# A transformer block with conditioning on one core: another order and other products in its front

## The chip, the cores and the metric

The kernel runs on one core of a Trainium2 chip. The metric is the time of one execution on the device in microseconds. The engines are named as the profile names them: PE (TensorE; PEld are its weight loads), DVE (VectorE), ACT (ScalarE), POOL (GpSimd) and SP (SyncE, which here only issues DMAs). A product in float32 on PE appears in the trace as two records.

## The reference

Two batches of 2048 tokens with 576 channels go through one block with 16 heads of 36 channels. A conditioning vector per batch gives six vectors (shift, scale and gate for the attention, shift, scale and gate for the MLP).

```python
ada = jax.nn.silu(c) @ W_ada + b_ada
shift_msa, scale_msa, gate_msa, shift_mlp, scale_mlp, gate_mlp = jnp.split(ada, 6, axis=-1)
h = _modulate(_layernorm(x), shift_msa, scale_msa)
x = x + gate_msa * _attention(h, W_qkv, b_qkv, W_proj, b_proj)
h = _modulate(_layernorm(x), shift_mlp, scale_mlp)
mlp = jax.nn.gelu(h @ W_fc1 + b_fc1, approximate=True) @ W_fc2 + b_fc2
x = x + gate_mlp * mlp
```

`_modulate(x, shift, scale)` is `x * (1 + scale) + shift`. Everything is float32.

## The kernel before

The kernel has a front and a main part. Each engine runs its instructions in the order in which the program gives them.

**The front** (lines 141 to 427) makes queries, keys and values of batch 0 and everything that comes from the conditioning. Channels are cut in five pieces of 128 (`kc`, the last with 64 channels and a row for the bias), tokens in four stages of 512 (`tb`). A stage is the generator `queries_keys_values` (L175): it loads four tiles of x (L180), takes mean and variance and normalizes them on DVE (L102 to L127, L190), turns them on PE so that channels lie on partitions (`pt`, L201), applies scale and shift while leaving PSUM (L136 on ACT, L138 on DVE) into `hT`, multiplies 9 tiles of queries and keys (`pq`, L208, 128 x 512, five products each) and four tiles of values (`pv`, L231), and stores them to `qk_d` and `v_d` in DRAM through SP's queue (L223, L248).

The conditioning comes from `c_in` (Silu, L265), turned into `cT` (five pieces with two columns, one per batch), and from W_ada, of which a sixth of 576 columns is one `wa` (`load_ada`, 1.33 MB, two buffers). `modulation(part)` (L282) makes scale or shift with the channels on partitions: for each of five output pieces and five `kc` one product with 128 x 128 weights of `wa` and the two columns of `cT` moving (`pa`, L288). `gates(part)` (L309) makes a gate with the same row on all partitions: weights `c_bc`, which is `cT` of one batch spread over 128 columns, and 288 columns of `wa` moving (`pg`, L318), ten products per batch. Parts 0 and 1 (shift and scale of the attention) are needed before the first `hT`; 2 and 5 are gates; 3 and 4 belong to the MLP. The gates then multiply W_proj and W_fc2, which go back to DRAM (`gated`, L335).

The order is written by hand: `next(stages[n])` advances a stage by one step, and the generator `later` (L363) is advanced once per tile of `pq` or `pv`, so that its work lies between them (L406 to L425). x is loaded through ACT's queue, W_ada through SP's, the first third of W_qkv (`w_in`) through POOL's and the others through SP's.

**The main part** (from L432) runs 128 units (one head of one block of 512 queries), each in four groups `G` of 256 + 256 keys: scores `s` (L496), copies to `e` (ACT, L509), maxima (DVE, L514), subtraction (L551), Exp (L555) and the product with the values `av` (L567). Scores run eight groups ahead of `av`. Beside this attention lies filling work, in steps of about 4 to 6 us of PE: `tokens` and `projections` for batch 1 (four times 512 tokens, `pq_q` L770, `pv_q` L732, their loads on POOL's queue), then for each finished block of queries its projection (`po` L887) and the MLP (`pf` L956 and L970, `py` L1020). `fill` takes steps from the list `work`. It is forced in every group before the first `av`, afterwards in every even group, and in an odd one if a credit allows it: the credit gains 2.55 in each group, loses the cost of each step, and starts at -10. Turns of tokens are `lights`: small steps, two of which may go into a group without a fill. At the start of the main part the first 512 tokens of batch 1 are normalized at once (L1075, with loads L636 and the norm L656 on ACT); their turns (`pt_q`, L677) are the first fills.

Of the kernel before, what the change touches and what calls it, by code (L numbers as in the profile page):

```python
# [10 lines left out]
F32 = mybir.dt.float32  # L11
# [11 lines left out]
def dit_block_kernel(  # L23
# [35 lines left out]
    def seq(ins):  # L59

        return tc.keep_in_program_order(ins)

    def rows(kc):
        return P if kc < KC - 1 else KL + 1
# [68 lines left out]
    def modulated(dst, pt, norm, kc, b, on_act):  # L133
# [3 lines left out]
        else:  # L137
            seq(nc.vector.tensor_scalar(dst, pt, sc, sh, op0=ALU.mult, op1=ALU.add))  # L138


    with ExitStack() as front:
        enter = front.enter_context
# [8 lines left out]

        evp = enter(tc.tile_pool(name="ev", bufs=4))
        wq_p = enter(tc.tile_pool(name="wqkv", bufs=1))
        hp = enter(tc.tile_pool(name="h", bufs=2))
        lnp = enter(tc.tile_pool(name="ln", bufs=4))
        ap = enter(tc.tile_pool(name="ada", bufs=1))
        awp = enter(tc.tile_pool(name="ada_w", bufs=2))
# [17 lines left out]
        def queries_keys_values(b, tb):  # L175
            mvs = lnp.tile([P, TB, nc.vector.BN_AGGR_DIM], F32, tag="mv", name=f"mv_{b}_{tb}", bufs=2)
            xts, xns = [], []
            for i in range(TB):
                xt = lnp.tile([P, C], F32, tag="xt", name=f"xt_{b}_{tb}_{i}", bufs=8)
                seq(nc.scalar.dma_start(out=xt, in_=x[b, ts(tb * TB + i, P), :]))  # L180
                xts.append(xt)
            yield
            for i in range(TB):
# [10 lines left out]
                )  # L194
                xns.append(xn)
            yield
            hT = hp.tile([P, KC, QB], F32, tag="hT", name=f"hT_{b}_{tb}")
            for kc in range(KC):
                pt = bank(f"pt_{b}_{tb}_{kc}")
                for i in range(TB):  # L200
                    seq(nc.tensor.transpose(pt[:, ts(i, P)], xns[i][:, ts(kc, P)], ident))  # L201
                modulated(hT[:, kc, :], pt, 0, kc, b, kc % 2 == 1)
            yield
            for m in range(2 * C // P):
                pq = bank(f"pq_{b}_{tb}_{m}")
                for kc in range(KC):
                    seq(
                        nc.tensor.matmul(  # L208
                            pq,
                            lhsT=w_in[: rows(kc), kc, ts(m, P)],  # L210
                            rhs=hT[: rows(kc), kc, :],
                            start=(kc == 0),
                            stop=(kc == KC - 1),
                        )
                    )
                ev = evp.tile([P, QB], F32, tag="ev", name=f"ev_{b}_{tb}_{m}")
                if m < C // P:
                    seq(nc.scalar.mul(ev, pq, SCALE))
                elif m == C // P:
                    seq(nc.vector.tensor_scalar_mul(ev, pq, qscale))  # L220
                else:
                    seq(nc.vector.tensor_copy(ev, pq))
                seq(nc.sync.dma_start(out=qk_d[b][ts(m, P), ts(tb, QB)], in_=ev))  # L223
                yield
            for i in range(TB):
                t = tb * TB + i
# [21 lines left out]
                seq(nc.sync.dma_start(out=v_d[b][ts(t, P), :], in_=vt.rearrange("p h e -> p (h e)")))  # L248
                yield

        stages = [queries_keys_values(0, tb) for tb in range(NQB)]
        next(stages[0])
        was = {0: load_ada(0), 1: load_ada(1)}
        w_in = wq_p.tile([P, KC, 3 * C], F32, name="w_in")
        main, last = pieces(w_qkv)
        for n in range(3):
            cols = ts(n, C)
            to = w_in[:, :, cols]
            by = nc.sync if n else nc.gpsimd
            seq(by.dma_start(out=to[:, 0 : KC - 1, :], in_=main[:, :, cols]))  # L260
            seq(by.dma_start(out=to[0:KL, KC - 1, :], in_=last[:, cols]))
            seq(by.dma_start(out=to[KL : KL + 1, KC - 1, :], in_=b_qkv[cols].unsqueeze(0)))
        next(stages[1])

        seq(nc.scalar.activation(c_in[:, 0:C], c_raw, AF.Silu))  # L265
        pt = bank("pt_c")
        for kc in range(KC):
            seq(nc.tensor.transpose(pt[:, ts(kc, B)], c_in[:, ts(kc, P)], ident[:B, :B]))
        cT = ap.tile([P, KC, B], F32, name="cT")
        seq(nc.vector.tensor_copy(cT.rearrange("p k b -> p (k b)"), pt[:, 0 : KC * B]))  # L270
        c_bc = ap.tile([P, B, KC, P], F32, name="c_bc")
        for b in range(B):
            for kc in range(KC):
                seq(
                    nc.vector.tensor_copy(
                        c_bc[:, b, kc, :], cT[:, kc, b : b + 1].to_broadcast([P, P])
                    )
                )

        def modulation(part):  # L280

            wa = was.pop(part)  # L282
            pa = bank(f"pa_{part}")
            for fc in range(KC):
                m = P if fc < KC - 1 else KL
                for kc in range(KC):
                    seq(
                        nc.tensor.matmul(  # L288
                            pa[:m, ts(fc, B)],
                            lhsT=wa[: rows(kc), kc, ds(fc * P, m)],  # L290
                            rhs=cT[: rows(kc), kc, :],
                            start=(kc == 0),
                            stop=(kc == KC - 1),
                        )
                    )
            to = 2 * (part // 3) + (1 - part % 3)
            add = 1.0 if part % 3 == 1 else 0.0
            spans = [(0, P, 0, KC - 1), (0, KL, KC - 1, KC)]
            if part // 3:
                spans.append((64, KL, KC - 1, KC))  # L300
            for at, m, lo, hi in spans:
                seq(
                    nc.vector.tensor_scalar_add(
                        mod[at : at + m, to, lo:hi, :].rearrange("p k b -> p (k b)"),
                        pa[:m, lo * B : hi * B],
                        add,
                    )
                )

        def gates(part, made):  # L310

            wa = was.pop(part)
            for b in range(B):
                pg = wide(f"pg_{part}_{b}")
                for n in range(2):
                    for kc in range(KC):
                        seq(
                            nc.tensor.matmul(  # L318
                                pg[:, n, :C2],
                                lhsT=c_bc[: rows(kc), b, kc, :],  # L320
                                rhs=wa[: rows(kc), kc, ts(n, C2)],
                                start=(kc == 0),
                                stop=(kc == KC - 1),
                            )
                        )
                g = ap.tile([P, C], F32, name=f"gate_{part}_{b}")
                seq(
                    nc.vector.tensor_copy(
# [1 line left out]
                    )  # L330
                )
                made.append(g)
                yield

        def gated(jobs):  # L335

# [27 lines left out]
        def later():  # L364
# [38 lines left out]
                at = slice(f, f + 3)  # L403
                jobs.append((src[:, at, :], P, 3, half, [d[:, at, :] for d in dsts]))
            yield from gated(jobs)
            modulation(3)  # L406
            yield
            modulation(4)

        next(stages[0])  # L410
        modulation(0)
        modulation(1)
        rest = later()
        next(rest)
        next(stages[0])
        for n, stage in enumerate(stages):
            if n + 2 < NQB:
                next(stages[n + 2])
            if n + 1 < NQB:
                next(stages[n + 1])  # L420
            for i, _ in enumerate(stage):
                next(rest, None)
                if i == 6 and n + 1 < NQB:
                    next(stages[n + 1])
        for _ in rest:  # L425
            pass
# [5 lines left out]
    with ExitStack() as main_part:  # L432
# [4 lines left out]
        ps_f = pool("ps_f", 2, space=PSUM)  # L437
        ps_v = pool("ps_v", 1, space=PSUM)
        ep = pool("e", 9)
        kp = pool("k", 2)  # L440
        np_ = pool("n", 2)
        bp = pool("blk", 2)
        mp = pool("mlp", 2)
# [2 lines left out]
        class Unit:  # L446
# [6 lines left out]
                self.es = {}  # L453

            def load_keys(self):
                u, b, h = self.u, self.b, self.h
                self.kT = kp.tile([P, HALF], F32, tag="kT", name=f"kT_{u}")
                self.qT = kp.tile([P, QB], F32, tag="qT", name=f"qT_{u}")
                for i in range(2):
                    at = ds(64 * i, D)  # L460
                    seq(
                        nc.sync.dma_start(
                            out=self.kT[at, :], in_=qk_d[b][ds(C + h * D, D), ts(i, HALF)]
                        )
                    )
                    seq(
                        nc.sync.dma_start(
                            out=self.qT[at, :], in_=qk_d[b][ds(h * D, D), ts(self.qb, QB)]
                        )
                    )  # L470

            def load_values(self):
                self.v = kp.tile([P, L // P * HA + 64 - HA], F32, tag="v", name=f"v_{self.u}")
                nt = L // P * HA
                seq(nc.vector.memset(self.v[:, nt:], 0.0))
                seq(
# [192 lines left out]

        def turned(key, xns, norm, b):  # L670

            h2 = bp.tile([P, KC, QB], F32, tag="big", name=f"h_{key}")

            def piece(kc):
                pt = room(f"pt_{key}_{kc}", 1)[0]
# [5 lines left out]


        lights = []
        ready = {}

        def lit():

# [134 lines left out]
        def gather(k):  # L822

            sums = bp.tile([P, H * QB // P], F32, tag="sums", name=f"sums_{k}")
            seq(nc.gpsimd.dma_start(out=sums, in_=flat_rows(sum_d[k])))
            oT = bp.tile([P, KC, QB], F32, tag="big", name=f"oT_{k}")
            outs[k] = oT
            seq(
                nc.gpsimd.dma_start(
# [239 lines left out]
        AHEAD = 2 * NG  # L1069
        RATE = 2.55  # L1070
        lasts = []
        work = [[tokens(1, tb), projections(1, tb), None] for tb in range(NQB)]
        credit = -10.0
        state["busy"] = True
        units[0].load_keys()  # L1075
        while work[0][0] is not None:
            if next(work[0][0], 0) == 0:
                work[0][0] = None

        def advance():  # L1080

# [149 lines left out]
```

## Time and profile before

| | us |
|---|---|
| median of 3 runs | 3847.03 (3845.86 to 3847.26) |
| the profiled execution: its time | 3850.33 |
| its span, on which the views below stand | 3848.6 |
| mean granted clock of PE | 0.991 |

"Span" is the time from the first to the last instruction in the trace. A busy time is the sum over the instructions of an engine. The chain is followed back from the last instruction: at each step to what released it. "Issue" in it is time in which the engine waited for nothing that the profile shows. The granted clock says which share of its full speed PE had.

### The profile page before, as it was taken

Reading aid. Unit: us, or ns where it says so; the run is one execution under the profiler, and the core shown is the slowest. Engines: PE = TensorE matmul, PEld = TensorE weight load, DVE = VectorE, ACT = ScalarE, POOL = GpSimd, SP = SyncE. Lnnn points to the kernel's source line nnn. Section 1 sums busy time; section 2 is a strip of 40 time slices with the busy share of each in tenths; the row PEclk is TensorE's granted clock in tenths of the full one; section 3 lists DMA queues with packets and bytes.
Section 4 is the critical chain, followed back from the end, with each engine's and each line's share of the span. In section 5 each row is a group of like instructions: output and inputs, shape, how many; then the busy total and the mean of one; then the engine's idle time right before and its main releaser. Section 6 shows DMA issues by size and latency. Waiting matters only on the chain.

```text
span 3848.6 us, 58305 instructions
## 1 busy us (share of the span) xinstructions
PE 3791.6 (99%) x23533; PEld 1806.7 (47%) x23533; DVE 2936.6 (76%) x2983; ACT 2340.9 (61%) x2203; POOL 568.5 (15%) x821
## 2 busy tenths in 40 slices
PE   8999999999999999999999999999999999999998
PEld 5554434444344444444444534454444444444555
DVE  2514787878888988898888898888888888888421
ACT  0003776766766776676776676667666767677321
POOL 0210111111111011111111021112110111011211
PEclk9998999999999999999999999999999999999999
DMA  5732443344444343343343343434342434243321
GB/s 167 255 136 69 87 99 94 87 116 88 104 86 93 69 95 85 85 88 88 69 102 90 70 112 69 99 71 105 74 102 63 105 80 93 68 102 63 104 82 57
DMA packets 415473, 362.60 MB, mean 94 GB/s; under 512 B 312762, under 2 KB 312762, under 8 KB 415204
## 3 DMA queue, kind: packets, MB, share of 16 engines
q1 hardware_dynamic: 350900, 173.37, 22.8%
q0 software_dynamic: 62000, 180.78, 15.6%
q10 hardware_dynamic: 2304, 4.72, 0.4%
q8 instruction: 186, 3.05, 0.4%
q14 instruction: 83, 0.68, 0.1%
HBM read 287.52 MB, written 71.21 MB: 93 GB/s over the span
## 4 chain that ended last, share of the span: by engine, by line
PE 93%; issue 4%; DMA 1%; DVE 1%; POOL 1%; ACT 0%; SPq 0%; POOLq 0%; ACTq 0%
PE av L567 23%; PE s L496 23%; PE py L1020 13%; PE pf L970 12%; PE pq_q L770 4%; PE pq L208 4%; PE po L887 4%; PE pv_q L732 2%; PE pv L231 2%; PE pf L956 2%; PE mt L532 2%; PE pa L288 1%; PE pg L318 1%; PE pt_b L677 0%; PE pt_q L677 0%
## 5 line engine op out<-in xcount | busy, mean ns | idle before, releaser
L509 ACT COPY e<-s 128x1024 f32<-128x1024 f32 x1024 | 989.7, 1024 | 690.4 <-PE s L496 688.7
L551 DVE TENSOR_TENSOR e<-e,m 128x2048 f32<-128x2048 f32 x512 | 1162.2, 2274 | 7.4 <-DMA m<-m_d 7.4
L514 DVE TENSOR_TENSOR acc<-acc,e 128x1024 f32<-128x1024 f32 x768 | 939.0, 1223 | 213.1 <-ACT e L509 169.0
L555 ACT ACTIVATE e<-e 128x2048 f32<-128x2048 f32 x512 | 992.0, 1938 | 9.4 <-DVE e L551 9.4
L567 PE MATMUL av<-e,v 64*64 64x512 f32 x8192 | 981.8, 594 | 0.6 <-DVE up L580 0.6
L496 PE MATMUL s<-qT,kT 36*64 36x512 f32 x8192 | 979.0, 592 | 0.8 <-ACT vt L245 0.8
L1020 PE MATMUL py<-w,gT 128*128 128x288 f32 x2304 | 585.1, 412 | 6.7 <-DVE gT L1000 3.5
L496 PEld LDWEIGHTS s<-qT,kT 36*64 36x64 f32 x8192 | 311.0, 133 | 561.7 <-issue 519.8
L567 PEld LDWEIGHTS av<-e,v 64*64 64x64 f32 x8192 | 291.5, 132 | 525.5 <-issue 475.5
L970 PE MATMUL pf<-h_b,w_b 128*128 128x512 f32 x1152 | 532.1, 606 | 4.4 <-DMA w_b<-in_L_cond_W_fc_dram 4.4
L1020 PEld LDWEIGHTS py<-w,gT 128*128 128x128 f32 x2304 | 434.4, 191 | 184.9 <-issue 36.8
L588 POOL DMA_DIRECT2D o_d<-up x128 | 110.0, 859 | 2239.2 <-DMA o_d<-up 1286.1
L970 PEld LDWEIGHTS pf<-h_b,w_b 128*128 128x128 f32 x1152 | 208.5, 190 | 323.6 <-issue 308.1
L542 DVE TENSOR_REDUCE mx<-mt 128x4 f32<-128x512 f32 x128 | 88.2, 689 | 200.5 <-PE mt L532 199.8
L981 ACT ACTIVATE gT<-pf,b 128x512 f32<-128x512 f32 x144 | 99.0, 687 | 189.7 <-PE pf L956 131.5
L887 PE MATMUL po<-wpr_p,oT 128*128 128x288 f32 (+1 forms) x640 | 167.9, 419 | 6.3 <-DVE x_b L899 6.3
L770 PE MATMUL pq_q<-h_q,w_q 128*128 128x512 f32 (+1 forms) x360 | 167.0, 611 | 6.5 <-DMA w_q<-in_L_cond_W_qkv_dram 6.5
L208 PE MATMUL pq<-hT,w_in 128*128 128x512 f32 (+1 forms) x360 | 161.8, 607 | 0.3 <-ACT hT L136 0.2
L514 DVE TENSOR_TENSOR acc<-e 128x1024 f32<-128x1024 f32 x128 | 155.4, 1214 | 4.7 <-ACT e L509 4.7
L992 DVE SCALAR_TENSOR_TENSOR th<-th,gT 128x1024 f32<-128x1024 f32 x72 | 88.1, 1223 | 90.9 <-ACT th L990 90.7
L887 PEld LDWEIGHTS po<-wpr_p,oT 128*128 128x128 f32 (+1 forms) x640 | 122.3, 195 | 62.4 <-issue 11.0
L1032 DVE TENSOR_TENSOR x_b<-py,x_b 128x288 f32<-128x288 f32 x192 | 81.5, 451 | 85.9 <-PE py L1020 85.8
(136 smaller groups left out, 2336.0 us busy)
## 6 DMA issues: line engine op xcount, KB each, us to landing
w<-w_d POOLq DMA_DIRECT2D x72, 576.0 KB, 6.2
v<-v_d SPq DMA_DIRECT2D x128, 296.0 KB
kT<-qk_d SPq DMA_DIRECT2D x256, 144.0 KB
w_b<-in_L_cond_W_fc_dram POOLq DMA_DIRECT2D x72, 512.0 KB, 4.5
m<-m_d SPq DMA_DIRECT2D x128, 256.0 KB
qT<-qk_d SPq DMA_DIRECT2D x256, 72.0 KB
w_d<-wg POOLq DMA_DIRECT2D x12, 864.0 KB, 6.3
qk_d<-ev SPq DMA_DIRECT2D x36, 256.0 KB
```

The costliest lines, as they stand in the source:

```text
L208: nc.tensor.matmul(pq, lhsT=w_in[: rows(kc), kc, ts(m, P)], rhs=hT[: rows(kc), kc, :], start=(kc == 0), stop=(kc == KC - 1),)
L496: nc.tensor.matmul(s[ts(c, 64), i, :], lhsT=self.kT[at, ds((2 * g + j) * P + 64 * c, 64)], rhs=self.qT[at, :], start=True, stop=True,)
L509: seq(nc.scalar.copy(self.es[g][:, j], s))
L514: top = lambda out, x, y: seq(nc.vector.tensor_max(out, x, y))
L551: seq(nc.vector.tensor_sub(e, e, m))
L555: seq(nc.scalar.activation(e, e, AF.Exp))
L567: nc.tensor.matmul(self.av[ts(i, 64), r, :], lhsT=self.v[ts(r, 64), ds((c + i * (HALF // P)) * HA, 64)], rhs=e[ts(r, 64), j, i, :], start= ...
L588: seq(nc.gpsimd.dma_start(out=o, in_=hi[1:HA, :], accum_op=ALU.add))
L770: nc.tensor.matmul(pq, lhsT=w[: rows(kc), kc, ts(j, P)], rhs=hT[: rows(kc), kc, :], start=(kc == 0), stop=(kc == KC - 1),)
L887: nc.tensor.matmul(po[n][:, :C2], lhsT=oT[: rows(kc), kc, ts(i, P)], rhs=wpr[: rows(kc), kc, ts(n, C2)], start=(kc == 0), stop=(kc == KC - 1),
L970: nc.tensor.matmul(pfs[j], lhsT=w1[:, kc, ts(j, P)], rhs=h2[:, kc, :], start=(kc == 0 and j == 0), stop=(kc == KC - 2 and j == 1),)
L1020: nc.tensor.matmul(py[n][:, :C2], lhsT=gTs[f - f % 2][:, f % 2, ts(i, P)], rhs=w2s[f - f % 2][:, f % 2, ts(n, C2)], start=(j == 0), stop=( ...
```

## The change

**The first loads.** x of the first two stages goes through SP's queue instead of ACT's, and so does the first third of `w_in` instead of POOL's. SP's order is then: the conditioning vector, x of stage 0, W_ada 0 and 1, `w_in` 0 and 1, x of stage 1, `w_in` 2, W_ada 2 and 5.

**The products of the conditioning.** `rows_of(part)` takes the two columns of `cT` as weights and 288 columns of `wa` as the moving side; the result is two rows (one per batch). The pieces `kc` 0 to 3 go to partitions 0, 32, 64 and 96 of the PSUM tile, so to four strips of 32 columns of PE; `kc` 4 is added to the first. The tile is cleared on DVE first, and copied to SBUF afterwards (`rows`). `modulation` then adds the strips up and turns the rows by five products with `rows` as weights and the two columns of `of_b` moving (`pm`). `gates` spreads them over all partitions by one product per half and batch with the weights `spread[b]`. `c_bc` goes.

**The order.** Between the rows of parts 0 and 1 and their `pm` the first two turns of stage 0 are issued. A gate takes the same number of steps of `later` as before (rows, then both batches); parts 3 and 4 take four steps instead of two. A fifth stage, `queries_keys_values(1, 0)`, is advanced up to its `hT`: the first 512 tokens of batch 1 are loaded (ACT's queue), normalized (DVE) and turned within the stages of the front, and the main part begins with `projections(1, 0)` without turns. The keys and queries of unit 0 are loaded after the last tile of `pq`. The buffers of `hT` and of the later `h` and `oT` are now one pool, as are the keys of the front and of the main part.

The diff, cut:

```diff
+    kp = ctx.enter_context(tc.tile_pool(name="k", bufs=2))
+    hp = ctx.enter_context(tc.tile_pool(name="h", bufs=2))
+    def load_keys(u):
...
-                seq(nc.scalar.dma_start(out=xt, in_=x[b, ts(tb * TB + i, P), :]))
+                by = nc.sync if (b, tb) in ((0, 0), (0, 1)) else nc.scalar
+                seq(by.dma_start(out=xt, in_=x[b, ts(tb * TB + i, P), :]))
...
+            pts = []
+            if (b, tb) == (0, 0):
+                pts = [turn(kc) for kc in range(2)]
+                yield
+            for kc in range(KC):
+                pt = pts[kc] if kc < len(pts) else turn(kc)
                 modulated(hT[:, kc, :], pt, 0, kc, b, kc % 2 == 1)
...
+                if m == 2 * C // P - 1 and tb == NQB - 1:
+                    first_keys.extend(load_keys(0))
...
-        stages = [queries_keys_values(0, tb) for tb in range(NQB)]
+        stages = [queries_keys_values(0, tb) for tb in range(NQB)] + [queries_keys_values(1, 0)]
         next(stages[0])
         was = {0: load_ada(0), 1: load_ada(1)}
...
+        load_in(0)
+        load_in(1)
         next(stages[1])
+        load_in(2)
+        NC = P // 32
+        of_b = ap.tile([P, B], F32, name="of_b")
+        nc.vector.tensor_reduce(
+            out=of_b,
+            in_=ident.rearrange("p (k q) -> p q k", k=NC)[:, 0:B, :],
+            op=ALU.add,
+            axis=AX.X,
+        )
+        def cleared(part):
+            pa = wide(f"pa_{part}")
+            seq(nc.vector.memset(pa[:, :, :C2], 0.0))
+            return pa
+        pas = {part: cleared(part) for part in range(2)}
...
+        def rows_of(part):
+            wa = was.pop(part)
+            pa = pas.pop(part) if part in pas else cleared(part)
+            for n in range(2):
+                for kc in range(KC):
+                    at = 32 * (kc % NC)
+                    seq(
+                        nc.tensor.matmul(
+                            pa[at : at + B, n, :C2],
+                            lhsT=cT[: rows(kc), kc, :],
+                            rhs=wa[: rows(kc), kc, ts(n, C2)],
+                            start=(kc < NC),
+                            stop=(kc == KC - 1 or 0 < kc < NC),
+                        )
+                    )
+            t = ap.tile([P, C], F32, tag="rows", name=f"rows_{part}", bufs=2)
+            seq(nc.vector.tensor_copy(t.rearrange("p (n c) -> p n c", n=2), pa[:, :, :C2]))
+            return t
+        def modulation(part, t):
+            pm = wide(f"pm_{part}")[:, 0, :]
             for fc in range(KC):
                 m = P if fc < KC - 1 else KL
-                for kc in range(KC):
-                    seq(
-                        nc.tensor.matmul(
-                            pa[:m, ts(fc, B)],
-                            lhsT=wa[: rows(kc), kc, ds(fc * P, m)],
-                            rhs=cT[: rows(kc), kc, :],
+                seq(
+                    nc.tensor.matmul(
+                        pm[:m, ts(fc, B)], lhsT=t[:, ds(fc * P, m)], rhs=of_b, start=True, stop=True
...
         def gates(part, made):
-            wa = was.pop(part)
+            t = rows_of(part)
+            yield
             for b in range(B):
                 pg = wide(f"pg_{part}_{b}")
                 for n in range(2):
-                    for kc in range(KC):
-                                lhsT=c_bc[: rows(kc), b, kc, :],
-                                rhs=wa[: rows(kc), kc, ts(n, C2)],
+                            pg[:, n, :C2], lhsT=spread[b], rhs=t[:, ts(n, C2)], start=True, stop=True
...
-            modulation(3)
-            yield
-            modulation(4)
+            for part in (3, 4):
+                t = rows_of(part)
+                yield
+                modulation(part, t)
         next(stages[0])
-        modulation(0)
-        modulation(1)
+        ts_ = [rows_of(part) for part in range(2)]
+        next(stages[0])
+        for part in range(2):
+            modulation(part, ts_[part])
+        for b in range(B):
+            seq(nc.vector.tensor_copy(spread[b], of_b[:, b : b + 1].to_broadcast([P, P])))
...
-        for n, stage in enumerate(stages):
-            if n + 2 < NQB:
+        for n in range(NQB):
+            if n + 2 <= NQB:
                 next(stages[n + 2])
-            if n + 1 < NQB:
-                next(stages[n + 1])
-            for i, _ in enumerate(stage):
+            next(stages[n + 1])
+            for i, _ in enumerate(stages[n]):
                 next(rest, None)
-                if i == 6 and n + 1 < NQB:
+                if i == 6:
                     next(stages[n + 1])
...
-        ready = {}
+        ready = {"q1_0": (hTs[1, 0], [])}
...
-        work = [[tokens(1, tb), projections(1, tb), None] for tb in range(NQB)]
+        work = [[tokens(1, tb) if tb else None, projections(1, tb), None] for tb in range(NQB)]
         credit = -10.0
         state["busy"] = True
-        units[0].load_keys()
-        while work[0][0] is not None:
-            if next(work[0][0], 0) == 0:
-                work[0][0] = None
+        units[0].kT, units[0].qT = first_keys
```

## The prediction

> **What bounds the kernel now.** First the page: its busy times, its clock row and the shares of the chain. TensorE is busy for all but 57 us.
>
> ```profile
> PE 3791.6 (99%) x23533; PEld 1806.7 (47%) x23533; DVE 2936.6 (76%) x2983; ACT 2340.9 (61%) x2203; POOL 568.5 (15%) x821
> ...
> PEclk9998999999999999999999999999999999999999
> ...
> PE 93%; issue 4%; DMA 1%; DVE 1%; POOL 1%; ACT 0%; SPq 0%; POOLq 0%; ACTq 0%
> ```
>
> So time is won only by giving PE less to do, by letting it start sooner, or by a higher clock. The change touches the front (to 323 us) and the first steps of the attention, so second I read the chain there, in order of time (start, length, what).
>
> ```profile
> 1.16 10.58 DMA wa<-in_L_cond_W_ada_dram
> 12.13 1.28 ACT L265
> ...
> 15.17 19.64 PE pa L288 x100
> ...
> 39.74 17.30 PE pq L208 x40
> 57.04 4.86 PE pg L318 x20
> ...
> 205.95 5.57 PE pa L288 x50
> 211.52 7.20 PE pq L208 x10
> 218.72 7.88 PE pa L288 x50
> 227.04 6.15 issue
> ...
> 327.26 1.62 ACT xn_q L656 x2
> ...
> 344.06 5.79 PE pq_q L770 x10
> 349.86 1.88 PE s L496 x16
> ```
>
> To see: the first useful product, pq, starts at 39.7 us; 100 narrow records of pa stand before it; pa for the MLP's parts takes 13.5 us around 206; the first pq_q of batch 1 starts 21 us after the front's end (the last pv ends at 323.4). Third, the windows of those stretches (width, PE busy and records, the other engines, granted clock, DMA share, GB/s).
>
> ```profile
> 206.00:207.00 1.00, 1.00 (x11) 1.00 (x10) 0.75 (x1) 0.00 (x0) 0.00 (x0) 1.00 1.06 389
> ...
> 212.00:213.00 1.00, 1.00 (x2) 0.33 (x1) 0.00 (x0) 0.00 (x0) 0.00 (x0) 0.50 0.00 0
> ```
>
> ```profile
> 335.00:340.00 5.00, 5.00 (x23) 1.85 (x22) 2.41 (x2) 3.06 (x4) 0.00 (x0) 0.50 0.00 0
> ```
>
> To see: pa runs 11 records in 1 us at clock 1.00; after 4.5 us of it the clock is 0.50, and the pq behind it takes 7.2 us instead of 4.29. The clock is 0.50 again from 326 to 346 us, as attention starts. In the windows from 16 to 24 us pa makes only 11 records in 2 us: half rate too, although no throttle is recorded yet.
>
> **Part A, the start: 10.9 us.** Today pa waits for the Silu, which stands on ScalarE behind the eight xt issues until 12.1 us. Those move to SP's queue. There the order is now c_raw, four xt (1.18 MB), wa 0, wa 1, w_in 0 (1.33 MB each), so each queue entry counts. The windows give 0.59 MB in the first 4 us and then 349 GB/s on average to 32 us (324 with SP's queue alone, 28 to 32 us, so one queue suffices): wa 0 has landed at 9.5 us, wa 1 at 13.3, w_in 0 at 17.1. VectorE clears two banks, copies cT at about 6 us and needs 8.5 us for the norm (today 16.5 to 25.0): 14.6 us. The new rows product of a part has 10 matmuls of 288 columns, 20 records; pg shows 0.243 us each (4.86/20). The four kc groups lie in four column strips. If strips overlap as the 64x64 tiles do (16 records of 512 in 1.72 us, 0.43 each in pq: fourfold), the longest strip holds 8 records, 1.94 us, and at half clock 3.9. I take half clock: rows end at 13.4 and 17.3 us. Then two turns (1.05), 20 narrow pm records at 0.182 (3.6) and the additions (0.4): 22.4; three turns and their modulations remain of today's 4.8 us, about 3.9: pq at 26.3, 13.4 us earlier. From that I take 2.5 us, because today's pq starts at full clock and here it follows narrow records (the 7.20 above is 2.9 too long). The copies of rows (0.76 like gate) lie beside turns. Bounds: serial strips at half clock, 9.7 us per part, put pq at 37.9, and with that slow pq the part loses 0.7; full clock throughout leaves wa 1 as the bound, pq at 22.8 us and 16.9 gained. I take 10.9, since av shows that strips with different moving data overlap.
>
> **Part B, the gates: 10.9 us.** Today 4 x 4.86 = 19.4 us of pg. After: two rows products, 2 x 1.94, four spreads of 4 records, 4 x 0.97: 7.8. [...] Six parts switch, two of them here: 0.7. [...] If strips are serial it is 5.1. Clears and copies are on VectorE (0.76 each for the copies; it is busy for 10 of the 50 us from 50 on), and each pg waits until after the next pq, 4.3 us, which covers the copy; without the cover 0.8 us each.
>
> **Part C, parts 3 and 4: 11.6 us.** From 205.95 to the next turn at 232.94 lie 27.0 us. After: two pq, 8.6; two rows, 3.9; 20 pm records at 0.11, 2.2; switches 0.7: 15.4. This rests on the clock staying up. [...] Here PE is not idle at all and is still throttled, after 4.5 us of two-column products. [...] Serial strips give 5.8, with the drops staying 3.
>
> **Part D, the first tokens of batch 1: 9.7 us.** Today from 323.36 to 349.79 us PE does four groups of s, 20 transposes and one pq_q: 26.4 us, waiting for the norm on VectorE and ScalarE (to 328.9 us) and at half clock. After: 0.83 us of wait for the last vt copy as today, 4 x 1.88, 4.29, and the transposes now in the front at the 4.05 us that the stage at 232.94 needs: 16.7. The norm, 8.5 us on VectorE, moves beside pv and pq of the third stage (VectorE has 4 of 50 us there; uncovered it would cost 8.5). Its four loads go from POOL's to ScalarE's queue; behind them wait evictions of pq, as behind the xt loads of every stage today. POOL is rid of those and of w_in 0; wpr and w_q follow earlier, hidden. On SP, kT and qT of unit 0 now wait for the last qk_d store ahead of the v_d stores, some 2 us (v_d lands in 2.11); v is read over 20 us later, so nothing waits. The first e copy waits for the last v_d store today too. If the clock drops anyway, D is 5.
>
> **The rest.** Three fill slots (five lights) leave the loop. Set side by side, the two instruction orders show fills 3 to 6 steps early at first; the credit takes this back, and from the second third of block 0 on the lead is 0 to 2, the last av beside the same piece of block 6. I set the rest at nothing, with 6 us either way: the 6.5 us wait of pq_q for w_q between the first two token blocks should go, since its POOL neighbours change, and an equal one come between the second and third.
>
> Sum 10.9 + 10.9 + 11.6 + 9.7 = 43.1. The profiled execution took 3850.3 us with 1.7 outside the span of 3848.6; it would become 3807.2. It is 3.3 above the median of 3847.0, so 3804 for the median.
>
> **Rivals.** Serial strips (20%): 128-row strips might share one stream, as every row feeds four. For it, no row shows this shape; against it, av. Then -0.7 + 5.1 + 5.8 + 9.7 = 19.9: 3827. Throttle stays (15%): products with two weight columns might count as idle whatever they stream; for it the half rate from 16 us on, against it that pa streamed only two columns. A 7, B 9, C 4, D 8: 28, so 3819. Slower (6%): the moved phase of fills against units lets each of the 128 unit ends wait for an eviction, as it now does now and then (av for up 0.6, pt_q for vt_q 0.6 us). At 0.6 each that is 77 us: 3881; it decides from 0.34 us per unit end (43.1/128). Against it: the credit restores the phase. The gains eaten by several small waits: 4%, 3845.
>
> **How the numbers follow.** My case has 55%, 3804, and its own bounds 3795 to 3815. The range takes in both middle rivals: 3792 to 3828. Measurement tells 0.2% (7.7 us). Faster 0.90 (55 + 20 + 15), same 0.04, slower 0.06.
>
> **What would show it.** A: first pq near 26 us, and rows records overlapping (20 in about 2 to 4 us). B: pg groups of 1 us. C: clock 1.00 around the two pm groups and no stretch of pq above 4.5 us. D: first pq_q within 4 us of the last pv, clock 1.00. I am wrong if rows takes 4.86 us or more, if the clock rows still show 0.50 in the front, or if PE's idle time after 350 us grows.

## The result, and the profile after

The changed kernel takes 3804.28 us (median of 4 runs, 3802.73 to 3805.81), the kernel before, on the same chip, 3847.15 (4 runs, 3845.86 to 3850.51): ratio 0.9885, 95% interval 0.9869 to 0.9901. A second comparison on another chip gave 0.9880 (0.9863 to 0.9896). The forecast was 3804. The profiled span fell from 3848.6 to 3802.8 us, by 45.8; the profiled execution of the kernel before was 3.2 us slower than the median of its kernel, that of the changed kernel 0.3.

The page after, the lines that answer to those shown of before (busy times, clock row, shares of the chain):

```profile
PE 3748.3 (99%) x23429; PEld 1762.1 (46%) x23429; DVE 2946.1 (77%) x2995; ACT 2335.5 (61%) x2196; POOL 564.7 (15%) x814
...
PEclk9999999999999999999999999999999999999999
...
PE 93%; issue 4%; DVE 1%; ACT 1%; DMA 1%; POOL 0%; POOLq 0%; SPq 0%; ACTq 0%; DVEq 0%
```

To see: TensorE's busy time fell by 43.3 us, the rest of the span by 2.5 (57.0 to 54.5). The change gives TensorE less to do and a faster clock (mean granted 0.995, before 0.991); TensorE still bounds the kernel (93% of the chain).

The chain of the changed kernel in order of time (start, length, what):

```profile
11.36 6.30 PE pa L331 x40
17.66 1.02 PE pt L218 x8
18.68 2.20 PE pm L349 x20
...
24.63 17.89 PE pq L233 x40
42.52 2.04 PE pa L331 x20
...
49.05 1.94 PE pg L375 x8
...
55.30 1.53 issue
56.83 2.10 PE pa L331 x20
...
181.97 1.59 issue
183.57 2.11 PE pa L331 x20
185.67 4.49 PE pq L233 x10
190.16 1.01 PE pm L349 x10
191.17 1.17 issue
192.34 3.28 PE pa L331 x20
195.62 4.96 PE pq L233 x10
...
298.44 4.49 PE pq_q L812 x10
```

To see: the first pq starts at 24.6 us and not at 39.7. A rows group of 20 records takes 2.04 to 2.11 us. The first pq_q of batch 1 starts 2.9 us after the front's end (295.56; s waits 0.83 us from there). And three pieces called issue, 1.53, 1.59 and 1.17 us, stand ahead of rows groups: no step of the prediction has them. The last rows group (3.28) and the pq behind it (4.96) are slow. A window there shows why, clock 0.56 (width, PE busy and records, the other engines, granted clock, DMA share, GB/s):

```profile
193.00:194.00 1.00, 1.00 (x12) 0.23 (x3) 0.00 (x0) 0.00 (x0) 0.00 (x0) 0.56 0.00 0
```

The parts of the forecast against the two profiled executions, in us gained:

| part | forecast | profile | how the profile's number is made |
|---|---|---|---|
| A, the start | 10.9 | 14.5 | pq from 39.74 to 24.63, less 0.6 for its first 40 records (17.30 to 17.89) |
| B, the gates | 10.9 | 9.5 | 57.04 to 89.37 is 32.3; 42.52 to 65.38 is 22.9 |
| C, parts 3 and 4 | 11.6 | 7.4 | 205.95 to 232.94 is 27.0; 181.97 to 201.58 is 19.6 |
| D, first tokens of batch 1 | 9.7 | 9.6 | 26.4 against 12.9 for the same work after the front and 3.9 for the turns in it |
| the rest | 0 (6 either way) | 4.8 | 45.8 less the four |

The total is within 3 us of the difference of the spans, but through terms that were off by up to 4.8 us in both directions. The experiments ask about each.

### The profile page after: what moved, and what is told of

It reads as the page before. It is cut to its first block, busy times and chain, and to the rows that moved or that the text cites. A ratio compares the mean times of both kernels' runs of the same rounds, so it can differ in the third digit from the quotient of the medians.

```text
span 3802.8 us, 58130 instructions
## 1 busy us (share of the span) xinstructions
PE 3748.3 (99%) x23429; PEld 1762.1 (46%) x23429; DVE 2946.1 (77%) x2995; ACT 2335.5 (61%) x2196; POOL 564.7 (15%) x814
## 3 DMA queue, kind: packets, MB, share of 16 engines
q0 software_dynamic: 61328, 178.27, 15.4%
## 4 chain that ended last, share of the span: by engine, by line
PE 93%; issue 4%; DVE 1%; ACT 1%; DMA 1%; POOL 0%; POOLq 0%; SPq 0%; ACTq 0%; DVEq 0%
PE av L609 23%; PE s L538 23%; PE py L1062 13%; PE pf L1012 13%; PE pq_q L812 4%; PE pq L233 4%; PE po L929 4%; PE pv_q L774 2%; PE pf L998 2%; PE pv L258 2%; PE mt L574 2%; PE pa L331 0%; PE pt_b L719 0%; ACT e L551 0%; DMA o_d<-up 0%
## 5 line engine op out<-in xcount | busy, mean ns | idle before, releaser
L631 POOL DMA_DIRECT2D sum_d<-up x128 | 143.6, 1122 | 0.0
```

What stands on the lines that cost most here:

```text
L631: seq(nc.gpsimd.dma_start(out=sums, in_=hi[0:1, :], accum_op=ALU.add))
```

## The experiments

Each kernel is the changed one with one edit, unless it says otherwise. A ratio to the kernel before has an interval of about 0.0015 either way, some 6 us; smaller differences are read from the traces. Most runs were on other chips than the first comparison, so the ratios are what compares; "above the changed kernel" means above 3804.28.

**Do the strips stream beside each other?** In rows_of all five kc groups go to one strip:

```diff
-                    at = 32 * (kc % NC)
+                    at = 0
...
-                            start=(kc < NC),
-                            stop=(kc == KC - 1 or 0 < kc < NC),
+                            start=(kc == 0),
+                            stop=(kc == KC - 1),
```

> The changed kernel, with all five kc groups of a rows product in one column strip, one after the other (the other three strips hold the zeros of the clear, so the sum is the same). My theory: a rows group of 20 records takes 2.1 us after the change because the four strips stream beside each other; on one strip each record takes the 0.243 us of pg, a group 4.86 us: 2.8 us more for each of parts 2, 5, 3 and 4 (11 us), and 8 to 13 us more at the start, where part 0 runs at half clock: 19 to 24 us above the changed kernel, 3824 to 3828. The rival, that the records are short because their weights have only two columns: a group stays at 2.1 us and the time at 3804.

Measured: 3821.82 us, ratio 0.9931 (0.9914 to 0.9947), 17.5 above the changed kernel. From its chain:

```profile
48.40 4.95 PE pa L331 x20
...
65.62 6.70 PE pa L331 x20
```

To see: the same 20 records take 4.95 us, 0.248 each like pg's, and 6.70 where the clock falls inside them (0.66, 0.50, 0.50 and 0.63 in the four windows from 66 to 70 us). Parts 3 and 4 take 5.01 and 6.70. The weights are as narrow as before, so the short group comes of the four strips side by side; the rival falls. The start loses 5.5 us (first pq at 30.13) and the four later groups 2.9, 4.6, 2.9 and 3.4: 19.3, and the first s of attention stands at 315.64, 19.25 later. The whole span differs by 17.3.

**The three waits named issue.** The timeline of the changed kernel at the second of them (start, length, engine, line, what, and in brackets the idle time before it):

```profile
182.06 0.75 DVE L245 TENSOR_SCALAR ev<-pq,qscale 128x512 f32<-128x512 f32 x1 [5.21 <-PE pq L233]
...
182.93 0.54 DVE L313 MEMSET pa<- 128x576 f32 x1
...
183.57 2.11 PE L331 MATMUL pa<-wa,cT 128*2 128x288 f32 x20 [1.61 <-issue]
```

To see: VectorE had waited 5.21 us for the pq tile, evicts it, and only then clears the bank, because `cleared(part)` stands behind that eviction in its queue; TensorE waits for both. The edit clears one step earlier, ahead of the eviction:

```diff
@@ gates(part, made, clear=None); part 2 is called with clear=5
+            if clear is not None:
+                pas[clear] = cleared(clear)
             yield
@@ later()
-            yield from gated(jobs)
+            steps = 2 + B * len(jobs)
+            for i, _ in enumerate(gated(jobs)):
+                if i == steps - 1:
+                    pas[3] = cleared(3)
+                yield
             for part in (3, 4):
                 t = rows_of(part)
+                if part == 3:
+                    pas[4] = cleared(4)
                 yield
```

> The changed kernel, with the clears of the PSUM tiles of parts 5, 3 and 4 one step earlier on VectorE's queue: ahead of the eviction of the pq tile that TensorE is still computing, not behind it. My theory: TensorE's waits of 1.53, 1.59 and 1.17 us before the rows of these parts are the 0.69 to 0.75 us eviction, the 0.54 us memset and their semaphores; all three go, 4.3 us; and if the clock drop from 192 to 198 us came of 1.0 us of pm, the 1.2 us wait and 2.1 us of rows in a row, it goes too, 1.6 us more: 3798 to 3800. Rival: TensorE waits there for something else (the bank, or the weights of the part from memory): no gain, 3804. The clock drop may stay, since pm and rows still follow each other: then 3800.

Measured: 3796.72 us, ratio 0.9864 (0.9849 to 0.9878). From its chain, parts 3 and 4:

```profile
182.85 4.49 PE pq L233 x10
187.34 0.99 PE pm L349 x10
188.33 2.04 PE pa L331 x20
190.37 4.49 PE pq L233 x10
```

To see: no issue piece stands between pm and rows, none is left ahead of the other two groups either (51.45 pq for 4.29 us, 55.74 rows), and rows and pq of part 4 are back at 2.04 and 4.49. Parts 3 and 4 now take 15.0 us (180.81 to 195.85), where the forecast had 15.4. So C's missing 4.2 us were these waits and the clock drop behind them. That the drop needs the wait is shown by more than one pair: in all five traced executions that have the wait ahead of part 4's rows (the changed kernel twice, serial strips, D taken out, old loads) the clock falls to 0.50 as it ends or within 1.3 us of that, in none of the four with early clears and single pm products. The first s of attention starts at 290.67 and not 296.39, although the first pq of this run was 0.44 later: 6.2 us from the clears.

**Part D taken out**: the first tokens of batch 1 are again normed and turned at the start of attention.

```diff
-        stages = [queries_keys_values(0, tb) for tb in range(NQB)] + [queries_keys_values(1, 0)]
+        stages = [queries_keys_values(0, tb) for tb in range(NQB)]
...
-        ready = {"q1_0": (hTs[1, 0], [])}
+        ready = {}
...
+        while work[0][0] is not None:
+            if next(work[0][0], 0) == 0:
+                work[0][0] = None
```

> The changed kernel without the first tokens of batch 1 in the front: they are normed and turned at the start of attention, as before the change; unit 0's keys are still loaded early. My theory: the front ends 3.9 us earlier and from its end to the end of the first pq_q group it takes about 26 us again, not 17, with clock 0.50: 9 to 13 us above the changed kernel, 3813 to 3817. The wait of pq_q for w_q falls between the first and the second token block again, about as long as now. A rival for the 4 to 5 us that were gained after the first blocks and that no part of my sum named: if they come of the phase that part D changed, they go too: 3818 to 3822, and the four waits of po for x_b (6.3 us) are back.

Measured: 3819.34 us, ratio 0.9923 (0.9908 to 0.9937), 15 above the changed kernel: the rival's number. From its table of waits (engine, line, for what: us in total, times, longest):

```profile
PE po L930 <- DVE x_b L942: 6.3, 4, 1.6
...
PE py L1063 <- DVE x_b L1075: 3.1, 2, 1.6
```

The po line of the pages of the kernel before and of the changed one (busy, mean ns, idle before it and what ended that):

```profile
L887 PE MATMUL po<-wpr_p,oT 128*128 128x288 f32 (+1 forms) x640 | 167.9, 419 | 6.3 <-DVE x_b L899 6.3
...
L929 PE MATMUL po<-wpr_p,oT 128*128 128x288 f32 (+1 forms) x640 | 163.0, 410 | 0.1
```

To see: the four waits of po and the two of py are back exactly as in the kernel before (6.3 and 3.1); in the changed kernel po does not wait for x_b at all, and py 1.6 us once. The clock is at half again as attention starts (10.0 us lost from 296 to 318 us), and the wait for w_q, 7.0 us, stands ahead of the third token block, not the second as I had written. So these waits come and go with D: with it, the fill steps meet the attention units at another phase, and the first steps of po no longer wait for VectorE. They account for part of the 4.8 us that no term of the sum named. After 350 us, TensorE's waits fell by 3.2 us in all (29.0 to 25.8), and the loss to half clock by 2.1 (12.8 to 10.7): 5.3 together. How much of that a usual execution would show stays open: the profiled one of the kernel before was 3.2 us above its median, and the interval of this run, some 6 us, does not separate 15 from the 9 to 13 of my first theory. The waits do.

**The old products** (old modulation, old gates with `c_bc`; new loads and D stay):

> The changed kernel with the old products of the conditioning (the weights of w_ada against two moving columns for the modulation, the broadcast conditioning against w_ada for the gates); its loads and its first tokens of batch 1 stay. My theory: the old pa needs 19.6 us for parts 0 and 1 from about 11.5 us on and the first pq starts at 36 to 37 us instead of 24.4, 12 us later; the gates cost 9.5 us more and parts 3 and 4 7.4 us more, with the clock at 0.50 behind pa: about 29 us above the changed kernel, 3833. Rival: the start was gained by the loads: then the first pq starts at 28 us or earlier and the sum is 17 to 20 us, 3822 to 3825.

Measured: 3828.24 us, ratio 0.9947 (0.9932 to 0.9961), 24 above. Its first pq starts at 35.1 us, 10.5 later (forecast 12), the gates take 32.3 us again (9.5 more), and the first s stands at 323.67, 27.3 us later. From its chain:

```profile
10.45 19.61 PE pa L324 x100
...
35.09 17.22 PE pq L233 x40
52.30 4.86 PE pg L354 x20
```

To see: pa takes as long as in the kernel before, though it starts 4.7 us earlier. The new products carry most of the start as well; the rival, 28 us or earlier, falls. The spans differ by 23.2 us and not by 27.3, because after the front this execution lost 6.6 us to half clock, the changed kernel's profiled one 10.7.

**The old loads** (x of two token blocks on ScalarE's queue, w_in 0 on POOL's; new products and D stay):

```diff
-                by = nc.sync if (b, tb) in ((0, 0), (0, 1)) else nc.scalar
-                seq(by.dma_start(out=xt, in_=x[b, ts(tb * TB + i, P), :]))
+                seq(nc.scalar.dma_start(out=xt, in_=x[b, ts(tb * TB + i, P), :]))
...
+            by = nc.sync if n else nc.gpsimd
```

> The changed kernel with its first loads as before the change: x for the first two token blocks from ScalarE's queue (eight issues ahead of the Silu), w_in 0 from POOL's, the rest from SP's. My theory: the new products need the loads too, since rows waits for the conditioning and the turns for the norm: the Silu comes at 13.4 us again instead of 3.7, x lands beside w_ada and the norm ends near 25 us, and the first pq starts near 30 us instead of 24.4: 5 to 6 us above the changed kernel, 3809 to 3811. Rival: one queue gives no more bytes than three, w_ada lands when it lands, and the start stays at 24 to 25 us: 3804.

Measured: 3811.20 us (3808.10 to 3816.31), ratio 0.9902 (0.9886 to 0.9919), 7 above, little more than the interval. From its timeline:

```profile
15.13 4.00 PE L325 MATMUL pa<-wa,cT 128*2 128x288 f32 x20 [0.26 <-DVE cT L316]
20.50 3.38 PE L325 MATMUL pa<-wa,cT 128*2 128x288 f32 x20 [1.37 <-DMA wa<-in_L_cond_W_ada_dram]
...
30.46 9.76 PE L232 MATMUL pq<-hT,w_in 128*128 128x512 f32 x19
```

To see: the conditioning is turned at 14.2 us again, rows run at 15.1 and 20.5, and the first pq starts 5.8 us later than in the changed kernel: the 5 to 6 us expected, not the rival's none.

**Narrow products and the clock.** On the kernel with early clears, pm of parts 3 and 4 computes each product eight times into the same place:

```diff
-            for fc in range(KC):
+            for fc in [f for f in range(KC) for _ in range(8 if part > 2 else 1)]:
```

> The kernel with early clears, in which each pm product of parts 3 and 4 is computed eight times into the same place (80 records of two columns in a row instead of 10). My theory of the clock: narrow products throttle a busy TensorE after about 4 us, so pm of part 3 takes 8 us at most for its first half and the rest at half speed, 12 to 14 us in all, with 0.50 in the clock rows inside it, although TensorE has no gap; the rows and pq behind it are slow as well; 22 to 30 us above the kernel with early clears. Rival, that only gaps without work lower the clock: 80 records at 0.10 to 0.11 us, 8 to 9 us, clock 1.00, 15 us above.

Measured in one execution: 3824.36 us, 27.6 above the kernel with early clears. From its timeline and its windows:

```profile
189.61 13.06 PE L349 MATMUL pm<-of_b,rows 128*128 128x2 f32 x80
```

```profile
192.00:193.00 1.00, 1.00 (x8) 1.00 (x8) 0.00 (x0) 0.00 (x0) 0.00 (x0) 0.62 0.09 31
193.00:194.00 1.00, 1.00 (x6) 1.00 (x6) 0.00 (x0) 0.00 (x0) 0.00 (x0) 0.50 0.00 0
```

To see: PE and its weight loads are busy all the time, and the clock falls to 0.50 some 2.5 us after pm began (189.77 to about 192.2), in the second group of 80 after some 2, and stays there to the end of the group. So narrow products lower the clock of a TensorE that has no gap, as I read from the old pa; the rival falls. The 4 us that I gave it are no fixed time: from the start of narrow products to the fall these traces have 1.6 us (old pa at 218.72, kernel before) to 4.3 (old pa at 201.22, old products). The last section has a finding on the moment.

**Three tries for more.** First, on top of the early clears, the first two turns between the rows of part 0 and part 1:

```diff
-        ts_ = [rows_of(part) for part in range(2)]
-        next(stages[0])
+        ts_ = [rows_of(0)]
+        next(stages[0])
+        ts_.append(rows_of(1))
```

> The kernel with early clears, in which the first two turns of token block 0 stand between the rows of part 0 and of part 1 instead of behind both. My theory: TensorE waits there for part 1 of w_ada in any case (about 1 us between the two rows groups), and the norm has ended by 13.8 us, so the turns cost nothing: the first pq starts 1.0 us earlier, 3795 to 3796. Rival: the rows of part 1 then start later, or the clock falls as before: no gain, 3797.

Measured: 3794.49 us, ratio 0.9856 (0.9841 to 0.9871), not to be told from early clears alone. The first pq starts at 25.37 us, against 25.07 and 25.64 in the two profiles without it: no gain. The rows of part 0 ended at 15.7 us in this run, so the turns ended at 16.7, and the rows of part 1, which began at 15.7 and 16.1 us in the two others, had to wait for that. Second, on top of that, the loads of w_q on SP's queue (in load_cols, `nc.sync` in place of `nc.gpsimd`):

> The same kernel as the run before, with the loads of w_q (the columns of the projection of batch 1) on SP's queue instead of POOL's. My theory of the 6.7 to 7.3 us wait of pq_q for w_q: its load stands on POOL's queue behind the store of a unit's output, which waits 20 us for that unit's last step; so on SP's queue the wait goes, and with it the clock drop of 2 to 3 us behind it: 9 us less, 3786 to 3788. Rivals: on SP's queue it stands behind the loads of m, which wait for the unit's maxima as well: then the wait stays, or a load of keys or of m comes late instead: 3795 or more.

Measured: 3796.26 us, ratio 0.9862 (0.9848 to 0.9877): no gain, my theory fell. The wait for w_q went from 6.8 to 5.4 us only. On SP's queue the load is issued at 408.0 us, right behind the loads of the next unit's keys and values, and its product could start at 409.3: it is asked for as its block begins. Whether an earlier request removes the wait was not tried. Third, the changed kernel and the one with early clears once more, side by side:

> The changed kernel once more, beside the kernel with early clears on the same chip, to compare the two: 0.9885 of the kernel before, within its interval, and the same three waits ahead of the rows of parts 5, 3 and 4 (4.3 us in all).

> The kernel with early clears once more, beside the changed kernel. My theory: 6 us below the changed kernel (the three waits of 4.3 us and the clock drop of 1.6 us in parts 3 and 4); what it was lower by beyond that in its first run (7.6 us in the times, 9.3 us in the profiled spans) is the chance of the short clock drops behind single waits later in the run, and differs this time. Rival: the early clears change something later as well, and it is 8 to 9 us below again.

Measured: 3803.04 us, ratio 0.9880 (0.9863 to 0.9896), and 3797.37 us, ratio 0.9869 (0.9853 to 0.9884): 5.7 us between the medians, as expected, with intervals that overlap. The profiled spans are 3802.3 and 3792.6. The same three waits (4.3 us) are in the first and not in the second. In the front alone the second is 9.2 us ahead this time (first s at 299.99 and 290.78), 4.3 of it by the waits. The rest is clock: in this run of the changed kernel it fell behind two of the three waits (in its first profile behind one), and at the start it was low for 6.8 us and not for 3.4. The traces show the 4.3 us of the early clears and the clock behind them; the intervals alone do not separate the two kernels.

**Part D alone** (old loads, old products):

> Only part D: the old loads and the old products of the conditioning, with the first tokens of batch 1 normed and turned in the front. My theory: the parts add up, and this one alone is worth what its removal cost, 15 us: 3832 to 3836 against 3847 before; the waits of po for x_b are gone here too. The first pq starts at 39.7 us as before the change. Rival: D gains only because the front ahead of it is short (the moved turns and norm collide with the late loads): 3840 or more.

Measured: 3833.82 us, ratio 0.9961 (0.9946 to 0.9976), 15.3 below the kernel before; first pq at 39.74, po without a wait for x_b. D alone is worth what its removal cost, each with an interval of some 6 us either way; the rival, 3840 or more, falls. Removed one at a time the three parts come to 7 (loads), 24 (products) and 15 (D), 46, against 43 for the change.

## Why the prediction was right, and where its steps were off

The mechanism was right in all four parts, and so was the sign; one cost, the clears, was left out. That 3804.28 came so close to 3804 is partly luck. By the profiled pair, A was 3.6 us too small, B and C together 5.6 too large, and the rest, put at nothing, 4.8 too small. By its own steps:

- **A, 10.9 forecast, 14.5 measured.** Rows ended at 17.66 us where I had 17.3, but by two errors that cancel: w_ada's parts came later (rows at 11.36 and about 15.3, where I had them landed at 9.5 and 13.3), and part 1's rows ran at full clock (2.3 us, not 3.9). The term that was mis-sized is pm, 3.6 by the old pa's half rate and 2.2 measured, and the 2.5 us deducted for a first pq at low clock, which were 0.6. Together 3.3 of the 3.6 us. Why pm ran at full rate: a trace lists the stretches of granted clock, and the first of them, 1.00, begins at 39.45 us in the kernel before, at 34.90 with the old products behind the new loads, and at 15.62 in the changed kernel. Ahead of that nothing is recorded, and the windows print 1.00 all the same, as they do in the stretch from 16 to 24 us whose half rate I had read. In the 19.6 us of the old pa no stretch begins; in the changed kernel one does 4.3 us after the first rows (11.36), and the last records of a rows group follow each other by 0.48 us in part 0 and by 0.24 in part 1. I had taken the half rate of the old pa for that of the place.
- **B, 10.9 forecast, 9.5 measured.** The four spreads (1.94 and 1.96 for two each) came as costed, rows (2.04 and 2.10) 0.26 us above the 1.94 each. The 0.7 us for the switches between rows and the products around them was an estimate from the attention of the kernel before (s or av behind pq_q 1.88 us and not 1.72, pq_q behind s 4.49, where pq behind pq takes 4.29); no run shows it by itself, and the profile after has in its place that 0.26 and 0.40 of the pq behind rows (4.49 us twice). What failed is the clear, which I put at nothing: the cover of a whole pq that I gave holds for the copies, not for it. I looked at VectorE's load, 10 of 50 us, and not at its order: the clear is queued behind the eviction of a tile that TensorE has only just finished, so it is late by eviction plus clear, however idle VectorE is. 1.53 us here against the 1.4 missing; part 2 escapes it, since the tile ahead of it is evicted by ScalarE.
- **C, 11.6 forecast, 7.4 measured.** The same clear: 1.59 and 1.17 us of waits. And that the clock stays up over 1.1 us of pm, my estimate from the 4.5 us of old pa that I read ahead of its fall (4.2 by the listed stretches), held for the last pm (0.99 us from 200.58, at 1.00), but pm, the wait and the rows made one stretch of little work (1.01, 1.17 and 3.28 us), and the clock fell at 193 us (1.2 us on rows, 0.5 on pq). With it one sign that I had named for being wrong came true, a clock of 0.50 in the front, and the pq of 4.96 us is longer than the 4.5 that I had allowed. Early clears gave 15.0 us for the stretch, where I had 15.4, with neither in it.
- **D, 9.7 forecast, 9.6 at its place.** But its removal, and its addition alone, move the time by 15. The rest, which I put at nothing, holds waits of po and py for x_b, which come and go with D through the phase of the fills; all of the 4.8 us is not shown to be theirs. I took the lead of 0 to 2 steps as no change; it changes which step stands at a block's beginning. The wait for w_q I had the wrong way round: in the kernel before it stands ahead of the third token block (pq_q at 644.0), in the changed one ahead of the second (422.8). It is as long, 6.5 and 7.3 us, so the sum did not feel it.
- **The rivals.** Serial strips: disproved; they would have cost 17.5, I had 23 (43.1 less 19.9). Throttle stays: half of it is true, narrow products do throttle a busy TensorE (80 pm records in a row, 0.50 with no gap), but the new groups (10 pm records, 0.99 us) are short enough while nothing waits between them (rows behind them 2.04 us with early clears). Slower by unit ends: TensorE's waits after 350 us fell from 29.0 to 25.8 us; one s waited for e, 2.3 us.

## What to carry to other kernels

Before calling a small step on an idle engine covered, find what it is queued behind: if that is the eviction of the tile that the busy engine has just finished, it is late by its own length and the eviction's (0.54 and 0.75 us here, a wait of 1.59), and moving it one step earlier cost nothing here. Use narrow products in short groups with broad ones between (10 pm records, 0.99 us, brought no fall of the clock in the runs with early clears, 80 brought 0.50), or let the narrow operand be the weights, in strips beside each other, and stream the wide one (20 rows records in 2.04 us, 4.95 in one strip). A piece taken out of a self-adjusting schedule changes what meets what for the rest of the run; bound that with an experiment, not with zero.

## What the runs showed of the hardware that I had not expected

A short wait can cost more than itself. In the kernel before, TensorE has six gaps of 1.57 us, some 405 us apart and once 503, where py or po waits for x_b. The windows at the first:

```profile
1209.00:1210.00 1.00, 0.00 (x0) 0.00 (x0) 1.00 (x2) 1.00 (x2) 0.00 (x0) 1.00 0.00 0
1210.00:1211.00 1.00, 0.62 (x1) 0.50 (x2) 1.00 (x3) 1.00 (x2) 0.00 (x0) 0.61 0.00 0
...
1213.00:1214.00 1.00, 1.00 (x4) 0.77 (x3) 0.00 (x0) 0.00 (x0) 0.00 (x0) 0.68 0.00 0
```

To see: TensorE is idle, the clock still 1.00; it falls to 0.50 as work resumes and is back at 1.00 within the last window, 3.4 us later (a share of 0.61 puts the fall at 1210.22, one of 0.68 the return at 1213.64). Some 1.6 us are lost on top of the wait. Five of the six gaps are followed by such a drop; in the kernel without the moved tokens, with the same six gaps, three. In the changed kernel the 1.53 us gap at 55.30 is followed by clock 1.00; the 1.59 us gap ahead of part 3's rows has clock 1.00 behind it in the first profile and 0.50 in the second, where the rows take 3.79 and not 2.11 us.

This looks like chance, but the stretches of granted clock that the thirteen traces list say more. In each trace all changes of the granted clock lie on one grid with steps of 3.41 us, from the first to the last (kernel before: 39.45 to 3845.31 us, 1115 steps of 3.4133; changed kernel: 15.62 to 3801.00, 1109; each change within 0.02 us of a step), and a low stretch lasts one to six whole steps (in the kernel before 3.41 us behind the gap at 1209, 20.48 us from 326.17; only the end of the execution cuts one short). Why they lie so is not shown. The traces hold 23 gaps of 1.57 us ahead of po or py. The ten that begin 1.0 to 2.1 us after a step of the grid are all followed by half clock; the thirteen that begin at most 0.55 us after one, or 2.25 us or more, are not. The late ones have 0.4 us or more of their length in the next step; why the early ones escape is not shown. The gaps ahead of the rows products lie on the same grid, but not within the same borders: the one at 55.30, 2.1 us after a step, had no drop.

Over the whole run half clock costs 31.0 us before and 14.0 us after (the shortfall of the granted clock times PE's busy time, over 2 us windows; the start, ahead of the first listed stretch, is not in it). Over a third of the 45.8 us between the two spans is clock, some of it by where gaps fell on the grid (behind gaps of 1.57 us five drops of 1.6 us before, none after).
